# Last layer of a four-layer network: when the sums over the scan's states, and their additions into y, are due in the issue order

## The chip, the cores and the metric

The kernel runs on one core of a Trainium2 chip. The metric is the device time of one execution in microseconds (us); several executions are timed, and their median is given. The profile is of one more execution on the same kind of core. TensorE is called PE (its weight loads PEld), VectorE DVE, ScalarE ACT, GpSimd POOL, and SyncE, whose queue issues all DMAs here, SP.

## The reference, cut to what matters

Input and output are 4 images of 192 channels by 56 x 56 pixels in float32. Three layers (a windowed attention with dynamic kernels, a frequency-channel attention, an overlapping-window attention with a gated convolution) come first. The change lies in the fourth, a selective scan in four directions:

```python
xn = _ln_cf(x, ln_w, ln_b)
xz = jnp.einsum('dc,bchw->bdhw', in_proj_w, xn)
xc, z = jnp.split(xz, 2, axis=1)
...
xs = jnp.stack([x_hw, x_wh, x_hw[..., ::-1], x_wh[..., ::-1]], axis=1)
x_dbl = jnp.einsum('kcd,bkdl->bkcl', x_proj_w, xs)
dts, Bv, Cv = jnp.split(x_dbl, [R, R + N], axis=2)
dt = jax.nn.softplus(...)
# per direction, along l:
dA = jnp.exp(dt_t[..., None] * A)
h = dA * h + dt_t[..., None] * B_t[:, :, None, :] * u_t[..., None]
y = jnp.einsum('bkdn,bkn->bkd', h, C_t)
...
y = ...  # the four directions added, plus Ds * xs
out = jnp.einsum('cd,bdhw->bchw', out_proj_w, _ln_cf(y) * jax.nn.silu(z))
return x + out
```

Each of the 192 channels has 4 states (n). The sum over the states, `h * C` over n, and the adding of its result into y are what the change moves.

## The kernel before

Layer 3 (the last) works through 4 images, 4 directions and 7 chunks of 448 pixels: 112 steps t, in the order of the list `steps`, and each in two halves h of 96 channels, so 224 half-steps. 32 channels times 4 states fill the 128 partitions, so a half-step has three groups j. One half-step is, by line:

- `load` (L2289, L2295): SP loads the step's dt rows and, spread over the partitions, the B and C rows (`bc`, 8 buffers).
- `sizes` (L2310, L2322): PE projects dt, ACT takes the softplus. It is done for two steps at once.
- `decay` (L2348, L2356): SP spreads dt over the states into a `da` buffer (10 of them), three per half-step; ACT takes the exponential in place.
- `scan`: DVE multiplies dt by u to `du` (L2371 for rows, L2374 for columns, strided); PE replicates it over the states into three banks of PSUM (L2381); DVE multiplies each by B in place (L2387); DVE scans each (L2403), from `da`, the bank and the last value of the step before; POOL multiplies the states by C into `da` (L2410). Then PE sums over the states into one bank, three products with a matrix of zeros and ones (L2426), which frees the three `da` buffers; and DVE adds that bank into y (L2431 in the first direction, L2436 for rows, L2440 for columns).

Around it run `begin` (layer norm, projections and a 3 x 3 convolution of the next image: L2079 to L2224, with the convolution in L2167 and its silu in L2184), and `final` (layer norm of y, gate product on POOL L2245, output projection L2254, residual L2265, store L2268). The layer norm's lines L2079, L2081, L2089, L2094, L2097, L2098, L2100 serve both. Layer norm needs the exponential's table set on ACT, `begin` that of silu, `sizes` that of softplus; a switch is a table load (L357).

Nothing of the order is left to a scheduler after the build. Every one of these pieces is a Python generator, a thread of the class `Order`, and the program is written in the order in which `Order.run` picks their steps. A step announces, by `yield on_pe(...)`, `on_dve(...)` and so on, its engine, an estimated cost, the buffers that it takes, the table set that it needs and, with `ready`, a time at which its inputs are there. `Order.start` gives the earliest time at which a step could run by that model: the engine free, the buffers free, and `ready`, or where that isn't given the end of the thread's last step plus 0.25. `Order.run` issues the step with the least such time (plus 0.05 for each place behind in the plan), and sets the engine's, the thread's and the buffers' times by it. `order.end` is the modelled end of the step issued last. On the chip each engine then takes its own instructions strictly in that order, and semaphores hold an instruction until its inputs are there. So a due time decides only what stands in front of what in each engine's queue.

The steps of the change stand at the end of `scan`. `on_pe(600, "bank")` costs the three sums 1.14 and lets them be due 0.25 after the modelled end of POOL's last product; `on_dve(448)` lets the addition be due 0.25 after the sums. Modelled costs are in the model's microseconds, and enter the program as order alone. There are 8 banks of PSUM; `take` and `done` keep the model's account of them and of the buffers.

Of the kernel before, what the change touches and what calls it, by code (L numbers as in the profile page):

```python
# [42 lines left out]
NS, DTR, SCH = 4, 12, 448  # L43
# [222 lines left out]
def rows2(ap, w=W):  # L266
    return ap.rearrange("p (y x) -> p y x", x=w)


class Order:  # L270
# [29 lines left out]
    def take(self, kind="bank"):  # L300
        slot = min((s for s in self.kinds[kind] if s[0] is not None), key=lambda s: s[0])
        slot[0] = None
        return slot[1]

    def done(self, tile):

        (slot,) = (s for slots in self.kinds.values() for s in slots if s[1] is tile)
        slot[0] = self.end + self.LATENCY
# [57 lines left out]
def on_pe(n, *takes, ready=None):  # L366

    return "PE", 0.0019 * n, takes, None, ready


def on_pe_us(us, *takes, ready=None):
    return "PE", us, takes, None, ready


def on_dve(*n, takes=(), ready=None, each=0.00105):
    return "DVE", sum(0.08 + each * i for i in n), takes, None, ready


def on_scan(n, ready):
    return "DVE", 0.1 + 0.0023 * n, ("st",), None, ready  # L380
# [6 lines left out]
def on_pool(*n, each=0.0011, takes=()):  # L387
    return "POOL", sum(0.2 + each * i for i in n), takes, None, None
# [1601 lines left out]
def layer3(tc, order, pools, src, packs, aps, dst):  # L1990
# [80 lines left out]
    def gone(*what):  # L2071
        return what in passed
# [258 lines left out]
    def use(t, h):  # L2331

        users[t, h] = users.get((t, h), 0) + 1
        if users[t, h] == 2:
            done(sized[t][0][h])
# [23 lines left out]
    def scan(t, h):  # L2359

        b, o, s, c = steps[t]
        head = c == (NSC - 1 if s else 0)
        last = c == (0 if s else NSC - 1)
        px = slice(c * SCH, (c + 1) * SCH)
        yield lambda: t in sized and (2 * t + h == 0 or gone("multiplied", 2 * t + h - 1))
        dts, b_, c_ = sized[t]
        u = us[b % 2]
        yield on_dve(SCH, takes=("du",), each=0.0018 if o else 0.0015)
        du = take("du")
        if o == 0:  # L2370
            nc.vector.tensor_mul(du, dts[h], u[:HALF, h, px])  # L2371
        else:
            uv = u[:HALF, h].rearrange("p (y x) -> p x y", x=W)[:, 8 * c : 8 * c + 8]
            nc.vector.tensor_mul(rows2(du, H), rows2(dts[h], H), uv)  # L2374
        use(t, h)

        yield on_pe(500, *["bank"] * 3)
        tiles = [take() for _ in range(3)]
        for j in range(3):
            r = slice(32 * j, 32 * j + 32)  # L2380
            nc.tensor.matmul(tiles[j][:, :SCH], w["c96.rep"][r], du[r], start=True, stop=True)  # L2381
        done(du)
        passed.add(("multiplied", 2 * t + h))
        ends = []
        for j in range(3):
            yield on_dve(SCH, ready=order.end if j else None)
            nc.vector.tensor_mul(tiles[j][:, :SCH], tiles[j][:, :SCH], b_)  # L2387
            ends.append(order.end + order.LATENCY)
        if h == 1:
            done(b_)  # L2390
        das, sts = [], []
        for j in range(3):
            g = 3 * h + j
            yield lambda: (t, h, j) in decays and (head or (t - 1, g) in states)
            da, at = decays.pop((t, h, j))
            yield on_scan(SCH, ready=max(at, ends[j]))
            sts.append(take("st"))
            r = slice(None, None, -1 if s else 1)
            first = 0.0
            if not head:  # L2400
                before = states.pop((t - 1, g))
                first = before[:, 0:1] if s else before[:, SCH - 1 : SCH]
            nc.vector.tensor_tensor_scan(  # L2403
                sts[j][:, r], da[:, r], tiles[j][:, :SCH][:, r], first, ALU.mult, ALU.add
            )
            done(tiles[j])
            if not head:
                done(before)
            yield on_pool(SCH, each=0.0024)
            nc.gpsimd.tensor_mul(da, sts[j], c_)  # L2410
            das.append(da)
            if last:
                done(sts[j])
            else:
                states[t, g] = sts[j]
        if h == 1:
            done(c_)
            del sized[t]

        yield lambda: b == 0 or gone("read", b - 1, c if (o, s) == (0, 0) else 0)  # L2420
        yield lambda: (o, s) == (0, 0) or len(started) == 2 * NSC * (b + 1)
        yield lambda: s == 0 or o == 1 or added[b] >= 6 * NSC + 2 * (NSC - 1 - c) + h
        yield on_pe(600, "bank")
        py = take()
        for j in range(3):
            nc.tensor.matmul(py[32 * j : 32 * j + 32, :SCH], w["c128.sum"], das[j], start=True, stop=True)  # L2426
            done(das[j])
        yield on_dve(SCH)
        sums = py[:HALF, :SCH]
        if (o, s) == (0, 0):  # L2430
            nc.vector.scalar_tensor_tensor(  # L2431
                y[:HALF, h, px], u[:HALF, h, px], d_sum[:, h : h + 1], sums, ALU.mult, ALU.add
            )
            started.add((t, h))
        elif o == 0:
            nc.vector.tensor_add(y[:HALF, h, px], y[:HALF, h, px], sums)  # L2436
        else:

            yv = y[:HALF, h].rearrange("p (y x) -> p y x", x=W)[:, :, 8 * c : 8 * c + 8]
            nc.vector.tensor_add(yv, yv, sums.rearrange("p (x y) -> p y x", y=H))  # L2440
        done(py)
        added[b] += 1
        if o == 0 and s == 1 and h == 1:
            passed.add(("summed", b, c))
        if added[b] == 8 * NSC:
            passed.add(("scanned", b))
# [12 lines left out]
    for t in range(len(steps)):  # L2459
        add(2 * t - 5, load(t))  # L2460
        if t % 2 == 0:
            add(2 * t - 3, sizes((t, t + 1)))
        for h in range(2):
            add(2 * t + h - 1, decay(t, h))
            add(2 * t + h, scan(t, h))
# [59 lines left out]
```

## Time and profile before

| | |
|---|---|
| runs | 5719.17, 5724.87, 5725.76 us; median 5724.87 |
| profiled execution | 5731.28 us, of which 5729.5 us are the span from its first to its last instruction |
| mean granted PE clock | 0.929 |
| busy over the span | PE 85%, DVE 72%, ACT 46%, POOL 30% |
| layer 3's scans (L2403) | 672, of 1133 ns (1073 ns for the first of a row of chunks) |
| sums (L2426) | 1344 matmuls, two for each of the 672 products, from 4006.6 to 5705.7 us |
| additions (L2431, L2436, L2440) | 56 + 56 + 112, of 666, 607 and 607 ns |

The profile has, for each line of the program and each engine, the time that its instructions were busy and the time that the engine stood idle just before them, with what ended that wait. The waits by pair (who waited for whom) add up such idle times. A busy share is an average over the stretch it is given for; an engine that is full in a stretch sets the pace there, and idle time of another costs nothing by itself. In a row of the windows, the numbers after the instruction counts are PE's granted clock, the mean share of the DMA engines, and GB/s.

### The profile page before, as it was taken

To read this page: it belongs to the slowest core of one execution; us is meant where nothing else is said; L and a number is where in the kernel's file an instruction comes from. 1 tells how busy PE (TensorE), PEld (TensorE's weight loads), DVE (VectorE), ACT (ScalarE), POOL (GpSimd) and SP (SyncE) were. 2 spreads that over 40 slices of the span, in tenths; PEclk is the share of its full clock that TensorE was granted. 3 is DMA by queue.
4 is the path that set the end of the run, shared out by engine and by line. 5 is a ranking of instruction groups with operands and counts; after the bars stand their busy time and mean duration, and the time that the engine had idled before them with its cause. 6 is when DMAs were issued, how large, how long until landed. Compare 5 with 4: busy or idle time off the path is not lost. (4 is left out here: it accounts for less than half of the span.)

```text
span 5729.5 us, 137267 instructions
## 1 busy us (share of the span) xinstructions
PE 4866.4 (85%) x58114; PEld 2407.0 (42%) x58114; DVE 4140.6 (72%) x6600; ACT 2655.4 (46%) x4271; POOL 1699.9 (30%) x1688
## 2 busy tenths in 40 slices
PE   4988998998899687898898888868888888888777
PEld 2444554454454444555555555534332232222112
DVE  5788447544744026888988888883678999998997
ACT  0122323212232215555555555546776776676544
POOL 0000000000000013433333433321345555555564
PEclk9999998999999798999999999989998999999998
DMA  6132224333332521000000000002456656566654
GB/s 185 53 80 60 66 60 105 64 88 91 76 69 56 99 77 37 14 22 21 17 22 18 19 20 21 16 26 60 122 135 157 160 145 172 155 149 167 165 149 109
DMA packets 356373, 475.97 MB, mean 83 GB/s; under 512 B 43600, under 2 KB 354256, under 8 KB 355248
## 3 DMA queue, kind: packets, MB, share of 16 engines
q1 hardware_dynamic: 355760, 467.20, 32.9%
q8 instruction: 458, 7.50, 0.5%
q14 instruction: 155, 1.27, 0.1%
HBM read 249.73 MB, written 63.17 MB: 55 GB/s over the span
## 5 line engine op out<-in xcount | busy, mean ns | idle before, releaser
L2410 POOL TENSOR_TENSOR da<-st,bc 128x448 f32<-128x448 f32 x672 | 857.0, 1281 | 751.5 <-DVE st L2403 600.1
L731 PE MATMUL bank<-X,wu 64*49 64x392 f32 x6720 | 610.5, 509 | 89.2 <-DVE X L710 85.9
L2403 DVE TENSOR_TENSOR_SCAN st<-da,st,bank 128x448 f32<-128x448 f32 x576 | 646.3, 1133 | 4.3 <-POOL da L2410 1.8
L838 POOL TENSOR_TENSOR attn<-attn,rs 112x1568 f32<-112x1568 f32 (+1 forms) x24 | 67.1, 2795 | 1726.5 <-DVE rs L836 989.9
L2356 ACT ACTIVATE da<-da,a_neg 128x448 f32<-128x448 f32 x672 | 410.1, 659 | 161.9 <-DMA da<-dt 150.2
L357 ACT ACT_TABLE_LOAD x373 | 478.6, 1283 | 6.6
L2387 DVE TENSOR_TENSOR bank<-bank,bc 128x448 f32<-128x448 f32 x672 | 382.9, 618 | 83.4 <-PE bank L2381 78.2
L731 PEld LDWEIGHTS bank<-X,wu 64*49 64x49 f32 x6720 | 247.6, 123 | 416.1 <-issue 366.4
L2426 PE MATMUL bank<-da,w_c 128*32 128x448 f32 x1344 | 348.8, 575 | 85.3 <-POOL da L2410 66.3
L2381 PE MATMUL bank<-du,w_c 32*128 32x448 f32 x1344 | 291.1, 643 | 105.2 <-DVE du L2371 59.2
L1569 DVE SCALAR_TENSOR_TENSOR bxn<-bapad,w_b,bxn 96x448 f32<-96x448 f32 (+2 forms) x448 | 318.7, 756 | 0.0
L1026 ACT ACTIVATE hm<-bank,w_a 128x448 f32<-128x448 f32 x168 | 106.3, 633 | 435.6 <-PE bank L1017 428.2
L1032 PE MATMUL bank<-hm,w_a 128*96 128x448 f32 x672 | 285.1, 555 | 16.7 <-ACT hm L1026 16.6
L1017 PE MATMUL bank<-xc,w_a 128*128 128x448 f32 x672 | 283.4, 551 | 0.6 <-DVE xc L998 0.6
L1430 POOL TENSOR_TENSOR bsq<-bsq 128x448 f32<-128x448 f32 (+7 forms) x120 | 144.5, 1206 | 446.9 <-ACT bsq L1427 401.8
L678 ACT ACTIVATE q<-bank,qk_bias,qk_scale 128x280 f32<-128x280 f32 (+2 forms) x216 | 116.9, 544 | 294.4 <-PE bank L664 251.2
L2134 PE MATMUL bank<-row,w_c 128*96 128x448 f32 x448 | 206.5, 599 | 29.7 <-DVE row L2100 27.9
L1488 PE MATMUL bank<-bxn,w_b 128*96 128x336 f32 (+2 forms) x576 | 214.3, 498 | 19.0 <-DVE bxn L1440 16.7
L754 ACT COPY sm<-bank 128x392 f32<-128x392 f32 x96 | 43.0, 489 | 380.6 <-PE bank L731 368.2
L2381 PEld LDWEIGHTS bank<-du,w_c 32*128 32x128 f32 x1344 | 92.1, 199 | 299.7 <-DVE du L2371 76.0
L998 DVE SCALAR_TENSOR_TENSOR xc<-bank,w_a,xc 96x224 f32<-96x224 f32 x112 | 44.9, 441 | 226.3 <-PE bank L988 124.5
L1763 PE MATMUL bank<-bzpad,b_diag 32*32 32x224 f32 (+2 forms) x8064 | 182.7, 371 | 24.1 <-ACT bzpad L1735 12.7
(333 smaller groups left out, 10015.4 us busy)
## 6 DMA issues: line engine op xcount, KB each, us to landing
da<-dt SPq DMA_DIRECT2D x672, 224.0 KB
vb<-vmem SPq DMA_DIRECT2D x576, 98.0 KB
bc<-prod SPq DMA_DIRECT2D x224, 224.0 KB
xq<-x SPq DMA_DIRECT2D x132, 210.0 KB
xc<-x SPq DMA_DIRECT2D x56, 336.0 KB
row<-x SPq DMA_DIRECT2D x56, 336.0 KB
xs<-x SPq DMA_DIRECT2D x28, 336.0 KB
vmem<-vt SPq DMA_DIRECT2D x56, 168.0 KB
```

The source lines that it names most:

```text
L357: self.nc.scalar.preload_act_table_set(table)
L731: nc.tensor.matmul(pm[a][outs[i], : WIN * W].rearrange("p (y x) -> p y x", x=W), wu[halves[a], k, dx], xt[halves[a], :, i, dx : dx + W], s ...
L1017: nc.tensor.matmul(ph[:, :CH], w["a128.c1T"][:, k, 128 * m : 128 * m + 128], xt[:, k], start=(k == 0), stop=(k == 1),)
L1032: nc.tensor.matmul(acc[h][:HALF, :CH], w["a128.c2T"][:, m, HALF * h : HALF * h + HALF], hm, start=(m == 0), stop=(m == 5),)
L1488: nc.tensor.matmul(rows2(pq[:HALF, :m]), w["b128." + wn][:, k, HALF * h : HALF * h + HALF], out[:, k], start=(k == 0), stop=(k == 1),)
L1569: nc.vector.scalar_tensor_tensor(dst, x, wt[:, t : t + 1], dst, ALU.mult, ALU.add)
L2356: nc.scalar.activation(da, da, AF.Exp, scale=a_neg[:, k, g : g + 1])
L2381: nc.tensor.matmul(tiles[j][:, :SCH], w["c96.rep"][r], du[r], start=True, stop=True)
L2387: nc.vector.tensor_mul(tiles[j][:, :SCH], tiles[j][:, :SCH], b_)
L2403: nc.vector.tensor_tensor_scan(sts[j][:, r], da[:, r], tiles[j][:, :SCH][:, r], first, ALU.mult, ALU.add)
L2410: nc.gpsimd.tensor_mul(da, sts[j], c_)
L2426: nc.tensor.matmul(py[32 * j : 32 * j + 32, :SCH], w["c128.sum"], das[j], start=True, stop=True)
```

## The change

The sums' step gets a cost of 0.85 in place of 1.14, and is due 3.0 after the modelled end of the step issued when it is announced (as a rule POOL's last product) in place of 0.25. The addition is due 1.5 after the modelled end of the sums in place of 0.25. No instruction and no buffer is added. Since the model goes on from there, `da` buffers and banks are free later by its account, and everything behind is placed anew, on all five queues.

```diff
         yield lambda: s == 0 or o == 1 or added[b] >= 6 * NSC + 2 * (NSC - 1 - c) + h
-        yield on_pe(600, "bank")
+        yield on_pe_us(0.85, "bank", ready=order.end + 3.0)
         py = take()
         for j in range(3):
             nc.tensor.matmul(py[32 * j : 32 * j + 32, :SCH], w["c128.sum"], das[j], start=True, stop=True)
             done(das[j])
-        yield on_dve(SCH)
+        yield on_dve(SCH, ready=order.end + 1.5)
         sums = py[:HALF, :SCH]
```

Before, the waiting conditions ahead of the sums (three `yield lambda` lines) set the thread's time to the present one plus 0.25; a given `ready` takes the place of that as well.

## The prediction

> **What bounds the kernel now.** The edit touches layer 3 alone, so I first asked in which stretch of the span its lines run (the sums, L2426, start at 4006.6 us and end at 5705.7 us), and then which engine is full there. The table of windows, microseconds of the window and then busy time and instruction count of PE, PEld, DVE, ACT and POOL:
>
> ```profile
> 4000.00:4400.00 400.00, 345.83 (x2937) 120.40 (x2937) 303.43 (x389) 291.71 (x459) 181.28 (x156) 0.90 0.54 135
> 4400.00:5600.00 1200.00, 982.10 (x6102) 300.12 (x6101) 1102.60 (x1429) 769.99 (x1183) 678.60 (x545) 0.93 0.61 157
> 5600.00:5730.00 130.00, 91.39 (x266) 28.27 (x262) 93.95 (x119) 53.81 (x80) 57.18 (x43) 0.83 0.40 106
> ```
>
> Stretch A (4000 to 4400) is shared: PE is busy 86%, DVE 76%. In stretch B (4400 to 5600) DVE is busy 92% and everything else has room: DVE is the bound, and its 97 us of idle time are all that an order of issue can win there. Stretch C is the end. So the second view is what DVE waited for, 4000 us to the end (total us, times, longest):
>
> ```profile
> DVE bank L2387 <- PE bank L2381: 74.0, 73, 3.3
> DVE row L2081 <- PE bank L2079: 43.9, 27, 8.7
> DVE y L2440 <- PE bank L2426: 26.7, 19, 5.3
> DVE y L2431 <- PE bank L2426: 20.6, 7, 12.8
> DVE row L2265 <- PE bank L2254: 20.3, 13, 7.0
> DVE y L2436 <- PE bank L2426: 13.1, 9, 2.7
> ...
> DVE st L2403 <- ACT da L2356: 8.1, 6, 2.9
> ```
>
> The three additions into y wait 26.7 + 20.6 + 13.1 = 60.4 us for the sums. The same view for B alone has 9.7 + 2.5 + 9.9 = 22.1 us of this, and 47.0 us at L2387. The scans hardly wait for their decays (8.1 us).
>
> Third, PE's side. A group from the page, and how it looks in PE's timeline (start, duration, what, idle before it):
>
> ```profile
> L2426 PE MATMUL bank<-da,w_c 128*32 128x448 f32 x1344 | 348.8, 575 | 85.3 <-POOL da L2410 66.3
> ```
>
> ```profile
> 5644.63 0.91 PE L2426 MATMUL bank<-da,w_c 128*32 128x448 f32 x2
> 5645.75 0.94 PE L2426 MATMUL bank<-da,w_c 128*32 128x448 f32 x2 [0.21 <-POOL da L2410]
> 5647.85 0.94 PE L2426 MATMUL bank<-da,w_c 128*32 128x448 f32 x2 [1.16 <-POOL da L2410]
> ```
>
> PE has reached the three sums too early and stands between them until GpSimd has done its next product; whatever is behind them in PE's queue stands too. PE loses 66.3 us so (58.1 in B, by its waits there).
>
> Last, the loop that the edit lengthens. A `da` buffer is free once its sum has run; then SP reloads it, ACT takes the exponential, DVE scans. The waits of SP's queue and of ACT, from 4000 us on:
>
> ```profile
> SPq L2348 <- PE bank L2426: 157.6, 135, 4.8
> ```
>
> ```profile
> ACT da L2356 <- DMA da<-dt: 150.2, 81, 5.7
> ```
>
> SP's reloads hang on the sums 135 times: later sums mean later decays.
>
> **The change part by part.** No instruction's work is changed: both programs have 29528 PE, 6602 DVE, 1693 POOL and 2622 SP instructions (as the program lists them). ACT has 4299 instead of 4266: 33 more table loads, 24 of them in the last quarter of the exponentials, where softplus and exponential now alternate by one chunk instead of two. The rest is order, and it changes a lot after the first scans. I counted, in DVE's issue order, the work standing between a producer and its consumer, each instruction at its mean from the page and the group view (scan 1.13 us, L2387 0.617, L2374 0.971, L2371 0.852, additions 0.61 to 0.67, L2081 1.08, L2100 1.06, L2265 0.60).
>
> (1) Third scan to its addition: 3.77 us of work between on average before, 7.00 after. The shortest real distance in the trace's B is 2.24 us (product, sums, addition). Below it are 28 of 224 additions before, lacking 29.8 us in sum; after, 8, lacking 6.0: 80% goes. In B the wait is 22.1 us, so 17.7 go. The other 38.3 us are in A and C, mostly A, where PE is the fuller engine and the 12.8 us wait ended after 28 matmuls of the column projections (L2218, 10.65 us in the chain of waits) had kept PE, not after a product of GpSimd; I take one third, 12.8 us (bounds 0 and 38).
>
> (2) du to the first L2387. The lack at 1.1 us (shortest distance in B: 1.11) grows from 14.2 to 22.3 us, as du is no longer so often followed by an addition. But PE now issues the next replication (L2381) ahead of more sums: two replications of later half-steps stand before a sum 99 times of 224, against 2 times before. Counting also the sums that stand just ahead of a replication, the lack goes from 28.7 to 26.4 us, by 8%. Of the 74.0 us that is 6 us of gain. Bounds: a loss of 19 (at 1.5 us the plain count goes from 27.3 to 45.9) and a gain of 37 (the B waits without the 10.5 us where PE began at once after du).
>
> (3) The other waits of DVE for PE (L2081, L2265, L2100: 15 us in B, some 23 in C) sit behind the same PE queue, freed of up to 58 us of standing. I take 5 us, bounds 0 and 25.
>
> (4) The `da` loop. From an addition to the next scan that uses one of its buffers there are 17.8 us of DVE work before (least 10.5), 14.3 after (least 6.4); since the addition also stands about 1.25 us further behind its sums, the loop loses 2 to 3.5 us. In B the exponential ends 7 to 8 us before its scan starts (mean; a tenth of the third scans have under 2.1 us). Which of these are bound by the buffer? Those whose ACTIVATE waited for the DMA: 87 exponentials, with 9.95 us to spare in the mean, and only 3 of them under 2.25 us, lacking 2 us together. If only those move, the price is 2 us; if every exponential moves by 2.25 us, the largest lack of each half-step adds up to 47 us, at 3.5 us to 113. I take 8, near the low end, because the low slack of the others comes from ACT's own order, which is built anew.
>
> (5) Table loads: 33 x 1.283 us = 42.3 us on ACT, which is busy 770 of 1200 us in B. Work hides it: exponentials are early by the 7 us above. Uncovered, it would cost up to 42 us.
> The row: before the 193 loads from 4000 us on ACT idled 3.5 us in all, and the exponential follows at once. The Trainium skill (ScalarE: Activation LUTs, What ACT_TABLE_LOAD costs) speaks against this edit more strongly: 1283 ns and a drain of some 1380 ns, 2.66 us for each switch. By it ACT would pay 88 us and not 42, an estimate from that page; this trace shows the load but no such idle time around it, so the sum goes by 42, hidden.
>
> (6) Collisions of DVE and GpSimd. The contiguous du product takes 0.59 us or up to 2.59:
>
> ```profile
> L2371 DVE TENSOR_TENSOR du<-dt,u x112: 590/596/2593, 3980.6 to 5685.8; 96x448 f32<-96x448 f32 x112
> ```
>
> In the timeline 17 of the 26 long ones start while GpSimd runs the 2.1 us gate product of `final` (L2245, 28 in all) and make 25 of the 28 us lost; the others start under an L2410. After the edit a du that follows a scan and one other instruction, where L2410 still runs, is found 16 times, before 6; the three of them in the trace that met no other product lost 0.5 us in the mean, so 5 us more. Whether L2245 meets du more or less often, an order of issue doesn't tell: 28 x 1.5 us is the most it could cost, 25 us the most it could give back. I take 0 for both together (bounds 25 gained, 42 lost).
>
> SP's queue is rearranged too (bc, dr and row loads move among the `da` reloads); the bc loads wait for GpSimd and L2387 as before, and I take nothing for it. A bank is held some 1 to 2 us longer per half-step; PE waits on DVE for banks little (L2426 <- L2403, 10.8 us in B). POOL keeps the same products.
>
> Sum: -17.7 - 12.8 - 6 - 5 + 8 = -33.5 us. The profiled execution took 5731.3 us (span 5729.5 and 1.8 around it), so 5697.8; it is 6.4 above the median of the runs, 5724.9, and on the median's scale the forecast is **5691 us**.
>
> **The rivals.** *The decays come late* (slower). Mechanism: the sums free `da` later, SP reloads later, ACT waits and, being in order, holds up softplus and layer norm as well, so all exponentials move, not just the 87. It decides once that shift passes some 2.1 us, where the lack (37 us at 2.0, 47 at 2.25) equals the 41.5 us gained. At 3.0 us it costs 84: 5725 - 41.5 + 84 = 5767. For it: least loop distance 10.5 to 6.4, all ten buffers in turn; against it: 9.95 us to spare where the DMA was the last to come. 20%.
> *The wait only changes its name* (no difference): additions stop waiting, but L2387 waits 18.6 us more by the 1.5 us count, A gives nothing: -17.7 + 18.6 - 5 + 8 = +4, or -9 with A's third: about 5722. For it: du and L2387 stand closer. 18%.
> *PE's standing was behind everything* (much faster): all 60 us of additions, 37 us of L2387 and some 15 of the others go, 8 lost: about -104, half of it likely: 5621 to 5672. Against it: no L2387 wait of B falls directly after a stand of PE at GpSimd. 12%.
> That the edit does nothing is excluded by the order.
>
> **How the numbers follow.** Forecast 50%, its own range 5672 to 5712 by the bounds of (1) to (4). The range 5650 to 5760 takes in the third rival's near half, the second, and most of the first. About 0.2% (11 us) is what a measurement can tell from no change. Faster by more: 50 + 12 less a little = 60%. Within: 18%. Slower: 22%.
>
> **What would show it.** Right: the additions' waits for L2426 fall from 60 to under 30 us; L2426's wait for L2410 falls well below 66; DVE busy share in B above 93%; L2403 waits for L2356 under 20 us. Wrong: L2403 <- L2356 at 40 us or more with ACT <- DMA da grown (first rival); L2387 <- L2381 at 90 or more (second). ACT loads 33 tables more in any case. The forecast is also wrong if L2371's busy time itself moves by over 10 us through (6).

## The result, and the profile after

The change makes the kernel slower: 5792.52 us, the median of 4 runs (5784.43 to 5796.60), against 5724.06 (5719.17 to 5725.76): ratio 1.0121, interval 1.0106 to 1.0136. The forecast of 5691 had the wrong sign, and the time lies above the range's end of 5760. The profiled execution took 5795.22 us (span 5793.4), 63.9 more than that of before; the parts below are counted in these two.

The table of windows of the changed kernel, the same first two windows as before, the third up to its later end (columns: window, length, busy time and count of PE, PEld, DVE, ACT, POOL, then granted clock, DMA share, GB/s):

```profile
4000.00:4400.00 400.00, 344.08 (x2979) 119.82 (x2978) 319.36 (x409) 288.64 (x461) 186.35 (x164) 0.91 0.55 140
4400.00:5600.00 1200.00, 930.95 (x5946) 295.04 (x5943) 1053.01 (x1345) 783.67 (x1172) 620.69 (x514) 0.82 0.59 149
5600.00:5795.00 195.00, 126.63 (x380) 37.98 (x380) 145.98 (x185) 86.10 (x123) 86.13 (x67) 0.76 0.45 112
```

In the first window DVE does 16 us more than before. In the second, where DVE is the bound, it falls from 92% busy to 88%, with fewer instructions done. PE didn't become full there either. Its clock fell from 0.93 to 0.82.

What DVE waited for, from 4000 us to the end (total us, times, longest):

```profile
DVE bank L2387 <- PE bank L2381: 145.4, 116, 4.9
DVE row L2081 <- PE bank L2079: 44.3, 33, 4.7
DVE row L2265 <- PE bank L2254: 28.6, 18, 7.0
DVE row L2100 <- ACT bank L2098: 15.5, 12, 4.0
DVE y L2431 <- PE bank L2426: 14.5, 6, 11.4
DVE y L2440 <- PE bank L2426: 8.0, 9, 2.1
DVE st L2403 <- issue: 6.6, 9, 1.4
DVE y L2436 <- PE bank L2426: 2.8, 4, 1.8
DVE st L2403 <- ACT da L2356: 2.2, 3, 1.2
```

The three additions wait 25.3 us in place of 60.4, and the scans 2.2 for their decays in place of 8.1. One row takes back more than all of this: the product behind the replication, L2387, waits 145.4 us in place of 74.0.

Two PE groups of the page (busy, mean ns; idle before, and the releaser that ended most of it):

```profile
L2381 PE MATMUL bank<-du,w_c 32*128 32x448 f32 x1344 | 325.1, 726 | 285.3 <-DVE du L2371 154.0
...
L2426 PE MATMUL bank<-da,w_c 128*32 128x448 f32 x1344 | 273.2, 655 | 18.6 <-DVE st L2403 11.6
```

The standing at the sums is gone, as intended: before, 85.3 us with 66.3 at POOL's product. But the replication, whose idle time was 105.2 us before (its row then: 291.1 busy, mean 643), now has 285.3 in front of it. The waits of PE between 4400 and 5600 us name the releasers, first before the change, then after:

```profile
PE bank L2426 <- POOL da L2410: 58.1, 82, 3.0
PE bank L2381 <- DVE du L2371: 42.6, 27, 3.8
PE bank L2381 <- DVE du L2374: 34.2, 33, 2.9
```

```profile
PE bank L2381 <- DVE du L2371: 116.8, 41, 5.8
PE bank L2381 <- DVE du L2374: 83.6, 34, 5.4
```

Once past the sums, PE arrives at the next replication and stands there for du: 200.4 us in place of 76.8. I read some 58 of these 124 us as the old standing under a new name: totals can't be matched piece by piece, but PE would have had to wait for DVE, the bound, in any case. PE's timeline in the last image shows it (start, duration, what, idle before it), before and after; before, PE waits for du (0.41 us at 5462.42) even behind the last of the sums:

```profile
5455.55 1.03 PE L2381 MATMUL bank<-du,w_c 32*128 32x448 f32 x6 [0.93 <-DVE du L2374]
5456.50 0.94 PE L2426 MATMUL bank<-da,w_c 128*32 128x448 f32 x2
5459.51 0.94 PE L2426 MATMUL bank<-da,w_c 128*32 128x448 f32 x2 [2.07 <-POOL da L2410]
5461.08 0.94 PE L2426 MATMUL bank<-da,w_c 128*32 128x448 f32 x2 [0.63 <-POOL da L2410]
5462.42 1.03 PE L2381 MATMUL bank<-du,w_c 32*128 32x448 f32 x6 [0.41 <-DVE du L2374]
```

```profile
5456.51 1.87 PE L2381 MATMUL bank<-du,w_c 32*128 32x448 f32 x6 [5.24 <-DVE du L2374]
5458.31 1.71 PE L2426 MATMUL bank<-da,w_c 128*32 128x448 f32 x6
5459.96 1.22 PE L2310 MATMUL bank<-dr,w_c 64*96 64x448 f32 x4
5464.28 1.87 PE L2381 MATMUL bank<-du,w_c 32*128 32x448 f32 x6 [3.11 <-DVE du L2374]
```

Before, a half-step's sums came one by one between two replications, and PE's idle time was cut into pieces of 0.4 to 2.1 us. After, the three sums are done in one go behind the replication, and the idle time is one piece of 3 to 5 us; and the replication takes 1.87 us in place of 1.03. The granted clock goes with the longer matmuls: by its record it was half at 5456.5 and at 5464.3 us after, and full at both replications before. This is the page's row of the granted clock in 40 slices, before and after:

```profile
PEclk9999998999999798999999999989998999999998
```

```profile
PEclk9999999999998889999999999889988988998658
```

The three slices before the last read 8, 6 and 5 in place of 9, 9 and 9.

Where the 63.9 us arise, by images of 168 scans each (length in us / granted clock):

| | image 0 | 1 | 2 | 3 (last) | behind it |
|---|---|---|---|---|---|
| before | 491 / .89 | 419 / .94 | 420 / .94 | 382 / .91 | 28.0 |
| after | 470 / .90 | 443 / .87 | 444 / .89 | 411 / .66 | 33.8 |

Image 0, where PE is the fuller engine, gains 21 us; each later image loses 24 to 29, and the end 6.

### The profile page after: what moved, and what is told of

The parts are those of the page before. It is cut to its first block, busy times and chain, and to the rows that moved or that the text cites. A ratio compares the mean times of both kernels' runs of the same rounds, so it can differ in the third digit from the quotient of the medians.

```text
span 5793.4 us, 137143 instructions
## 1 busy us (share of the span) xinstructions
PE 4849.1 (84%) x58114; PEld 2407.3 (42%) x58114; DVE 4158.3 (72%) x6600; ACT 2698.3 (47%) x4304; POOL 1674.3 (29%) x1688
## 5 line engine op out<-in xcount | busy, mean ns | idle before, releaser
L2410 POOL TENSOR_TENSOR da<-st,bc 128x448 f32<-128x448 f32 x672 | 829.4, 1243 | 812.1 <-DVE st L2403 657.6
L2381 PE MATMUL bank<-du,w_c 32*128 32x448 f32 x1344 | 325.1, 726 | 285.3 <-DVE du L2371 154.0
L2387 DVE TENSOR_TENSOR bank<-bank,bc 128x448 f32<-128x448 f32 x672 | 387.5, 620 | 150.2 <-PE bank L2381 149.7
L2356 ACT ACTIVATE da<-da,a_neg 128x448 f32<-128x448 f32 x672 | 408.0, 658 | 139.6 <-DMA da<-dt 138.1
L2381 PEld LDWEIGHTS bank<-du,w_c 32*128 32x128 f32 x1344 | 98.2, 219 | 495.1 <-DVE du L2371 160.5
L2426 PE MATMUL bank<-da,w_c 128*32 128x448 f32 x1344 | 273.2, 655 | 18.6 <-DVE st L2403 11.6
L2134 PE MATMUL bank<-row,w_c 128*96 128x448 f32 x448 | 205.5, 599 | 19.3 <-DVE row L2100 17.9
```

Source lines behind the costliest of these rows:

```text
L2356: nc.scalar.activation(da, da, AF.Exp, scale=a_neg[:, k, g : g + 1])
```

## The experiments

Ratios are to the kernel before, run again beside each group (its medians were 5718.0 to 5720.4), with their intervals. Three theories stood at the start. *The model's account* (theory A): with later sums the model believes the `da` buffers and banks to be free later, and so places all else worse. *The clock* (B): the fused idle time of PE lowers its clock, and slower replications make DVE wait. *The sums' own place* (C): they now stand in front of later replications in PE's queue. Every kernel that changes a number of the model or of the buffers gets a whole new order.

**Two more `da` buffers, after (e1) and before (e2).** In each: `keep_late("da", [SCH], 10)` becomes

```diff
-        da=keep_late("da", [SCH], 10),
+        da=keep_late("da", [SCH], 12),
```

> The change, with 12 da buffers in place of 10. Theory A (the later due sums keep the 10 da buffers taken in the model's account; the decays and scans are placed later, less DVE work is left between du and the first multiply by B, and ACT switches tables more often): with 12 buffers the model is not short of them, the work between du and L2387 lacks 47 us at 2.0 us (80 after, 52 before), loads fall from 407 to 383, so L2387 <- L2381 falls from 145 to under 80 us and the time to 5680 to 5705, faster than before. Theory B (PE's clock: with its stands at the sums gone PE waits for du in one longer piece, the granted clock falls, and the way from du over the replication to the multiply gets longer): clock after 4400 us stays under 0.85, time 5765 to 5795. Theory C (the sums' own place in front of later replications): L2387 waits stay above 120 us, time 5760 to 5795.

Measured: 5758.11 us, 1.0065 (1.0045 to 1.0084). Last image 392 us at clock 0.70; L2387 waits 119.7 us.

> The kernel before, with 12 da buffers: the control of the run with 12 buffers and the change. If two more buffers are worth time by themselves: 5690 to 5715. By theory A they are not, as the scans wait for decays only 8 us; the order that the model makes of them even has more lack between du and L2387 (93 us at 2.0 us in place of 52): 5725 to 5765. Theories B and C say nothing of it; the clock in the last image should stay about 0.9.

Measured: 5778.92 us, 1.0104 (1.0079 to 1.0128): 60 us slower than before, though the sums are due at once. Its last image took 418 us at clock 0.72, where about 0.9 was expected. More buffers are not better by themselves, so the 34 us of e1 can't be put down to them.

**The model's account alone (e3).** The sums stay late, but the model is told that the `da` buffers are free as early as with prompt sums:

```diff
             done(das[j])
+            order.free(das[j], order.end - 2.2)
```

`free` is a new method that only sets the slot's time. It enters the model alone; semaphores guard the buffer as before.

> The change with 10 buffers, but the model is told that the da buffers are free when they were in the kernel before (2.2 earlier than the end of the sums); the chip's own waits are untouched. Theory A: the order is like that with 12 buffers (lack 47 us at 2.0, 373 loads, third scan to addition 7.35 us), so 5690 to 5720, with up to 20 us of waits of L2403 for decays that are late in fact. Theory B: clock low, 5765 to 5795. Theory C: 5760 to 5795. If what costs the time is that the real buffers come late: L2403 <- L2356 over 40 us and the time above 5780.

Measured: 5758.90 us, 1.0068 (1.0051 to 1.0085). L2387 waits 106.9 us, last image 391 us at 0.72. It gives back nearly half of the loss, like e1; whether by its mechanism or as another throw of the order was then open (see the scatter below).

**Idle products for the clock, three places (e4; e5, e6; e9 to e11).** Products whose results nobody uses keep PE active in the last image; no step of the computation is left out, and the model isn't told, so the order of all else stays. First, four ahead of the sums:

```diff
         py = take()
+        for _ in range(4 if b == B - 1 else 0):
+            nc.tensor.matmul(py[:HALF, :384], ones, inT[:, 0], start=True, stop=True)
```

> The change, with four idle products of PE (constant operands, written into the sums' bank before the sums) ahead of the sums of the last image alone, which keep PE busy. The order is otherwise the same. Theory B: the clock of the last image rises from 0.52 to above 0.8, L2381 -> L2387 waits in it fall, and most of the 28 us lost there come back: 5760 to 5775. Theories A and C: the clock may rise, but the waits hang on the order: 5785 to 5800.

Measured: 5826.92 us, 1.0186 (1.0171 to 1.0201). The clock of the last image rose to 0.90, but the image took 453 us: the sums now came behind the idle products, and the additions waited 54 us.

Then five behind the sums, into unused rows of the bank, in the changed kernel and in the one before:

```diff
+        for _ in range(5 if b == B - 1 else 0):
+            nc.tensor.matmul(py[HALF:, :384], w["c128.sum"], inT[:, 0], start=True, stop=True)
         yield on_dve(SCH, ready=order.end + 1.5)
```

> The change, with five idle products of PE (constant operands, into partitions of the sums' bank that nobody reads) behind the sums of the last image's half-steps, where PE next waits for du; the order of all else is untouched. If the low clock (0.66 in the last image, 0.91 before) is what costs the last image its 29 us: the clock there rises above 0.85, the replication takes 1.2 to 1.4 us in place of 1.78, the L2387 waits of the image that start with PE ready fall from 22 to about 8 us, and the image takes 390 to 398 us in place of 411; in all 5773 to 5781. If the order alone does it: image 408 to 418 us and 5788 to 5800 in all.

Measured: 5816.93 us, 1.0164 (1.0149 to 1.0180); image 443 us at 0.90.

> The same five idle products in the kernel before, whose last image already has a clock of 0.91: a control of what they cost where the clock has little to gain. 0 to 10 us more than before, 5718 to 5728; if it is 20 us or more, the idle products are themselves in the way and the run with the change and these is read against that.

Measured: 5823.16 us, 1.0174 (1.0159 to 1.0190); image 482 us. In e5 the clock rose, in e6 it had little to gain, and both images grew longer. The additions' waits of e5 and of e6 show one reason (L2429 is the idle product):

```profile
DVE y L2442 <- PE bank L2429: 23.1, 14, 3.0
```

```profile
DVE y L2442 <- PE bank L2429: 58.5, 28, 3.5
```

The additions waited for the idle products themselves, which write other rows of the same bank. So these three runs measure their own waits too.

Last, three ahead of the replication, into the bank that it then overwrites, so that nothing but PE itself waits for them:

```diff
+        for _ in range(3 if b == B - 1 else 0):
+            nc.tensor.matmul(tiles[0][:32, :384], w["c128.sum"], inT[:, 0], start=True, stop=True)
```

> The change, with three idle products of PE ahead of each replication of the last image, written into the bank that the replication then overwrites: they run while PE waits for du, and no addition waits for them (in the runs before it did). If PE's long idle pieces and the half clock behind them cost the last image time: its clock rises from 0.66 above 0.85, the replication falls from 1.78 to about 1.3 us, its L2387 waits from 30 to 12 to 18 us, and the image from 411 to 390 to 400 us; in all 5772 to 5782. If the low clock is only a sign of a slow order: clock up, image still 408 us or more, 5788 or more.

> The same three idle products in the kernel before, the control: its clock in the last image is 0.91, so little is to be won, and PE's idle pieces are short, so they can delay the replication. 5720 to 5745, the last image 382 to 402 us.

> The change, with three idle products ahead of each replication of the last image and two ahead of those of the other images. If the lost clock (0.87 to 0.89 in images 1 and 2, 0.94 before) makes their 24 us each: clock 0.93, images 1 and 2 at 430 us or less, 5745 to 5770 in all. If it is the sums that stand in front of the replication when du is done: the idle products add 0.6 us to a PE that is already late 20 to 30 times of 56, images 1 and 2 at 443 us or more, no gain on the run with the last image alone.

Measured: 5787.29 us, 1.0120 (1.0103 to 1.0137), for the changed kernel; 5749.35, 1.0055 (1.0035 to 1.0075), for the one before; and 5872.23, 1.0263 (1.0244 to 1.0282), for the changed one with three in the last image and two in each of the others. The windows of the last image, before the change, after it, and e9:

```profile
5319.00:5701.00 382.00, 279.33 (x871) 67.20 (x870) 362.20 (x472) 189.72 (x280) 228.77 (x174) 0.91 0.58 150
```

```profile
5349.00:5759.00 410.00, 276.05 (x869) 72.47 (x870) 369.69 (x470) 216.88 (x300) 211.59 (x174) 0.66 0.56 137
```

```profile
5342.00:5751.00 409.00, 321.27 (x1199) 92.57 (x1198) 369.84 (x471) 219.73 (x302) 212.20 (x174) 0.90 0.56 137
```

The clock is back (0.66 to 0.90), the three replicated banks take 1.25 us again in place of 1.78 (1.16 before the change), and the image takes as long as ever. Inside it the L2387 waits with PE ready at once fell from 22 to 11 us, and those with PE late (it began the replication after du was ready) rose from 7 to 22: an idle product in front of a replication delays it where du is already there. In the kernel before, where the clock had little to gain (0.91 to 0.95), the same products cost 30 us of the image. So a high clock alone doesn't bring the time back. How much the low one cost, this can't say: if it did cost time, the remedy cost about as much. The control e10 was itself 10 us longer in the last image than expected (412 against at most 402), and in e11 images 1 and 2 have a clock of 0.93 and 0.95 and still take 471 and 468 us.

**Each half of the change alone (e7, e8, e12).** The sums late and the addition as before:

```diff
-        yield on_dve(SCH, ready=order.end + 1.5)
+        yield on_dve(SCH)
```

> Half of the change: the sums due later (cost 0.85 and 3.0), the addition due as before. If the loss comes from the sums' place in PE's queue (ahead of later replications, held da buffers, PE idle in longer pieces): nearly all of it is here, 5770 to 5800, L2387 waits above 120 us, clock of the last image under 0.75, 416 table loads. If it comes from the addition's place on DVE: 5710 to 5735.

Measured: 5839.08 us, 1.0202 (1.0176 to 1.0229). The addition 1.5 later, the sums as before:

```diff
-        yield on_dve(SCH)
+        yield on_dve(SCH, ready=order.end + 1.5)
```

> The other half: the addition due 1.5 after the sums, the sums due as before. DVE work from the third scan to the addition is 4.75 us (3.77 before, 7.00 after), the lack between du and L2387 at 2.0 us is 66 (52 before, 80 after). If the sums' place carries the loss: 5700 to 5730, additions wait 35 to 50 us in place of 60, the clock as before. If the addition's place carries it: 5760 or more.

Measured: 5709.53 us, 0.9986 (0.9976 to 0.9996). DVE's waits from 4000 us on, the sums alone and then the addition alone:

```profile
DVE bank L2387 <- PE bank L2381: 117.2, 109, 3.5
DVE y L2440 <- PE bank L2426: 38.6, 37, 2.8
...
DVE y L2431 <- PE bank L2426: 30.6, 15, 12.4
```

```profile
DVE bank L2387 <- PE bank L2381: 85.7, 75, 3.0
...
DVE row L2265 <- PE bank L2254: 31.4, 15, 7.0
DVE row L2100 <- ACT bank L2098: 22.9, 16, 2.2
DVE y L2431 <- PE bank L2426: 10.5, 11, 3.2
DVE du L2371 <- ACT dt L2322: 10.0, 1, 10.0
DVE y L2440 <- PE bank L2426: 9.8, 7, 2.1
...
DVE y L2436 <- PE bank L2426: 1.5, 2, 1.3
```

This is the separation. The later addition alone takes the additions' waits from 60.4 to 21.8 us, as much as the whole change does, and raises L2387 little (85.7; 74.0 before). The later sums alone make L2387 wait 117 us and don't help the additions (80.7 us). So what the change wins at the additions comes from its second line, and the loss from its first. By images it is the same: e8 alone shortens image 0 (461 us; 491 before), and e7 alone makes images 1 to 3 longer by 33 to 39 us. Two limits: the halves don't add up (+119 and -11 us, together +68), and e8's gain in time is small, because most of the 38.6 us come back in other rows: L2265 waits 31.4 us in place of 20.3, L2100 22.9 in place of 6.3, one du 10.0, and L2387 11.7 more. With the addition due 3.0 later:

> The kernel before, with the addition alone due 3.0 after the sums (the sums due as before). Third scan to addition 6.55 us of DVE work, as in the change, lack between du and L2387 at 2.0 us 28 (52 before, 66 with 1.5), 373 table loads. If the additions' place is harmless and the sums' place alone does the harm: additions wait under 20 us, L2387 under 75, clock as before, 5670 to 5700. If an addition that stands late blocks banks or the scans: 5715 or more.

Measured: 5714.93 us, 0.9991 (0.9982 to 1.0000). No more to gain there; 5670 to 5700 was expected if the additions' place were worth its waits.

**The scatter of the order (f1 to f4).** Since every new number makes a new order, I changed one that says nothing: the due time by 0.1 to 0.2, the modelled cost of prompt sums by 5%.

```diff
-        yield on_pe_us(0.85, "bank", ready=order.end + 3.0)
+        yield on_pe_us(0.85, "bank", ready=order.end + 2.9)
```

> The change with 2.9 in place of 3.0 in the sums' due time: a step in the model far smaller than any latency on the chip, but the issue order comes out anew (lack between du and L2387 at 2.0 us 71 in place of 80, 409 table loads). If the loss belongs to sums that are due late: 5775 to 5810. If much of it is the luck of one order: it moves by 25 us or more, out of that range.

> The same with 3.2 (lack 68, in the last image 12 in place of 27, 409 loads). If the loss belongs to sums that are due late: 5765 to 5805, the last image nearer 392 than 411 us as its lack is smaller. If much is the luck of one order: outside.

Measured: 5753.21 us, 1.0060 (1.0042 to 1.0077), for 2.9 and 5767.66, 1.0088 (1.0073 to 1.0103), for 3.2.

```diff
-        yield on_pe(600, "bank")
+        yield on_pe(570, "bank")
```

> The kernel before with the sums' modelled cost 570 in place of 600 (1.08 in place of 1.14), due as before: the order comes out anew (lack 62 in place of 52, 366 loads). If the loss of the change belongs to the late due time, this stays near before: 5710 to 5735. If one order's luck is worth tens of us: 5745 or more, or 5695 or less.

> The kernel before with the sums' modelled cost 640 (1.22), due as before (lack 68, 378 loads). As the run with 570: 5710 to 5740 if the late due time makes the loss, further off if one order's luck does.

Measured: 5700.65 us, 0.9968 (0.9958 to 0.9979), for 570 and 5723.01, 1.0009 (1.0000 to 1.0018), for 640. So three orders with prompt sums lie from 5701 to 5723, three with sums due about 3.0 later from 5753 to 5793. The groups don't overlap (30 us between their nearest), but inside each the order alone moves 22 to 40 us. The other runs fit: with prompt sums e8, e12 and f6 (below) took 5694 to 5715 us, with late ones e1, e3 and e7 5758 to 5839. One doesn't: e2, prompt with two more buffers, took 5779, so an order can be as slow without late sums. The change's own 68 us are the far end of these three; its typical price is some 50 (medians 5768 and 5718). And the 34 us that e1 and e3 gave back lie within this scatter: they show nothing of the model's account.

**Half the delay (f5), and the better half with another cost (f6).**

```diff
-        yield on_pe_us(0.85, "bank", ready=order.end + 3.0)
+        yield on_pe_us(0.85, "bank", ready=order.end + 1.5)
```

> The change with the sums due 1.5 after POOL's product in place of 3.0; cost 0.85 and the addition's 1.5 as in the change. The orders with the sums due at once took 5701 to 5723 us, those with 2.9 to 3.2 took 5753 to 5793. If the loss grows with the due time: between them, 5725 to 5760, PE's idle pieces of 2 us and more in the last image between 15 and 30, its clock between 0.7 and 0.9. If a small delay is harmless and only one that comes up to the next replication hurts: 5700 to 5725.

Measured: 5741.39 us, 1.0036 (1.0022 to 1.0049), between the groups; last image 392 us at 0.77. Last, the kernel before with cost 570 for the sums and the addition due 1.5 later:

> The fastest order so far (the kernel before with the sums' cost 570) with the addition alone due 1.5 later. If the additions' place gains by itself (60 us of waits gone to some 20): 5680 to 5698. If the gain of 18 us with 570 was the luck of one order: it is lost in a new order, 5700 to 5725.

Measured: 5694.46 us, 0.9952 (0.9939 to 0.9965), which beats both kernels. Its waits of DVE and the window of its last image:

```profile
DVE bank L2387 <- PE bank L2381: 98.0, 83, 3.0
...
DVE y L2431 <- PE bank L2426: 4.6, 2, 3.2
...
DVE y L2440 <- PE bank L2426: 1.2, 1, 1.2
...
DVE y L2436 <- PE bank L2426: 0.3, 1, 0.3
```

```profile
5286.00:5673.00 387.00, 279.14 (x882) 67.87 (x881) 360.47 (x473) 192.59 (x284) 227.70 (x175) 0.90 0.59 147
```

The additions wait 6.1 us, and the clock stays at 0.90: the additions' waits can be removed without late sums. Of its 25 us, 18 are what f3 has by the cost alone, a throw of the order; the other 7 are less than the scatter. Nor does the total at L2387 rank the kernels by itself: it is 98.0 us here, in the fastest, and 91.7 in e2.

**PE's idle pieces and its clock, over all runs.** Counted from the traces in the last image, PE with its weight loads:

| sums due | kernels | idle pieces of 2 us and more | us at half clock |
|---|---|---|---|
| at once | before, e8, e12, f3, f4, f6 | 7 to 14 | 61 to 82 |
| 1.5 later | f5 | 25 | 177 |
| about 3.0 later | after, e1, e3, e7, f1, f2 | 24 to 39 | 218 to 276 |
| at once, 12 `da` buffers | e2 | 40 | 236 |

Few long pieces go with a high clock and many with a low one, in each kernel without idle products; e2, slow with prompt sums, is in the pattern of the late ones. But the total idle time separates these groups as well (96 to 106 us at once, 116 to 156 about 3.0 later), and f5 and the change, with 130 us idle and 25 and 24 such pieces each, have 177 and 276 us at half clock. So the pieces alone don't set it.

The traces' clock records show more. The clock isn't halved more often: 16 times in the last image before the change, 15 times after. What differs is how long the half clock lasts. With the sums due at once its longest stretch there is 7 to 10 us, with f5 20, with the late sums 24 to 171, with e2 48; after the change it is one of 170.7 us, from 5463.9 us on. Its reason, as far as the records tell it, is in the last section.

## Why the prediction was wrong

Times of the whole stretch from 4000 us on, of the two profiled executions:

| step | foretold | measured |
|---|---|---|
| (1) additions wait for the sums | -30.5 | -35.1 (60.4 to 25.3) |
| (2) L2387 waits for the replication | -6, bounds -37 and +19 | **+71.4** (74.0 to 145.4) |
| (3) L2081, L2265, L2100 | -5 | +17.9 (43.9 to 44.3; 20.3 to 28.6; 6.3 to 15.5) |
| (4) decays | +8 | -5.9 (8.1 to 2.2) |
| (5) table loads | 0, hidden | no wait found that needs them (see below) |
| (6) du beside POOL | 0 | +12.8 (L2371 +4.8, L2374 +8.0) |

Together +61 of the 63.9 us.

**The step that failed is (2)**: "the lack goes from 28.7 to 26.4 us, by 8%. Of the 74.0 us that is 6 us of gain." In its place +71.4 us were measured. That the late sums make this wait is shown by e7 (117 us) against e8 (86); how, the traces tell in part.

- It took PE's standing at the sums as harm to what is behind them. What was behind was mostly a replication that had to wait for du. PE's waits for du in front of L2381 grew by 124 us as the 58 us of standing went, and L2387 waits more, not less.
- It took the chain from du to the first replicated bank as fixed at 1.1 us, the shortest distance of the old trace. That is still the shortest after, but in the last image the chain is mostly longer: the first bank takes 0.98 us in place of 0.71 and all three 1.78 in place of 1.16. A distance measured at one clock was used for an order that has another.
- Its bound of +19 came from trying 1.5 us for the chain. A sharper doubt was at hand: by the same count at 2.0 us, the lack goes from 52 to 80. Even those 28 us are less than half of the 71. Nor does its own range, 5672 to 5712, follow "by the bounds of (1) to (4)": at their bad ends (-17.7, 0, +19, 0, and 47 for the decays) they add up to 5773.

How much of the 71 us the clock carries isn't settled. In the last image (29 us longer) some 30 half-steps stall at L2387; at 0.27 to 0.62 us more for each replication that is 8 to 19 us, by direct count. In images 1 and 2 (24 us longer each) the clock fell less, to 0.87 and 0.89, and the waits there with PE late rose from 18 to 30 and 32 us: other PE work stood in front of the replication. In image 0 they rose as much, from 23 to 39 us, with the clock unchanged (0.89 and 0.90), so there the order does it without the clock. How the rise of images 1 and 2 divides stays open; e11, meant to tell, added its own work to the queue.

The other steps. **(1)** was right, in size and in place: from 4400 to 5600 us the additions' waits fell from 22.1 to 6.3 us (17.7 foretold to go), elsewhere from 38.3 to 19.0 (12.8). By e8 it is the work of the second line alone. **(3)** assumed PE to be freed, which it was not; 9 of its 18 us are L2100 behind ACT, on which the 33 more table loads of **(5)** (373 to 406, as foretold) lie. But they aren't needed for it: e8, e12 and f6 have 194, 193 and 184 loads from 4000 us on (193 before), and L2100 waits 22.9, 16.9 and 21.7 us there. So nothing here speaks against hidden loads. **(4)** was wrong in sign but small. In **(6)** the contiguous du moved 4.8 us, within the bound; the strided one, which it had not looked at, moved 8.0 us. Its group (shortest, median and longest in ns, then when), before and after:

```profile
L2374 DVE TENSOR_TENSOR du<-dt,u x112: 946/970/1012, 4134.5 to 5574.9; 96x448 f32<-96x448 f32 x112
```

```profile
L2374 DVE TENSOR_TENSOR du<-dt,u x112: 948/974/1671, 4127.4 to 5627.5; 96x448 f32<-96x448 f32 x112
```

The shortest and the median hardly change, the longest goes from 1012 to 1671 ns: a few of them, counted in the last section, are held up for long.

The rivals. *The decays come late*: refuted. SP waits longer for the sums (157.6 to 215.0 us), but ACT waits less for its reloads (150.2 to 138.1) and the scans less for ACT. *The wait only changes its name*: this was the right place, and its mark of 90 us at L2387 was passed with 145.4. Its price, 18.6 us, was a quarter of the true one, so that it ended at no difference. *PE's standing was behind everything*: refuted, and with it the belief that the forecast shared in part. Of the marks, the additions (25 us), the sums' wait for POOL and the decays came out as foretold; DVE's share above 93% did not (88%), and that was the one that stood for the time.

## What to carry to other kernels

An engine that stands in its queue for a result loses nothing by it if what comes next would have waited too: before moving the standing instruction back, look up what the instruction behind it waits for. If only the consumer was too early (the additions on the bound engine), move the consumer and leave the producer; here the addition alone got all that the change won at the additions. That is still no gain in time by itself: where the bound engine meets other waits soon after, most of it comes back there. And where an issue order is made by a model, change a number that says nothing first: the scatter of the order, 22 to 40 us here, is the least that a difference must exceed before one order against another shows a cause.

## What the runs showed of the hardware

- The granted clock follows how busy PE was in the 3.4 us before. In the clock records of these traces it is 1 or 0.5, in pieces that are whole multiples of 3.41 us. I counted such windows in all 20 profiled runs, from 4000 us to the last scan, with the busy time of PE's matmuls. After a window at full clock with PE busy for less than 40%, the next was at half clock in all 747 cases; at 60% or more, in 137 of 6449. After a window at half clock with PE busy for less than 80%, the clock never came back (652 cases); at 97% or more it did in 1035 of 1119. So idle pieces of about 2 us can be enough to halve the clock, and it takes a much fuller window to get it back: in the last image 35 of 81 windows at half clock were under 80% after the change, 1 of 20 before. In images 1 and 2, pieces of 1.5 us and more go from 9 in each to 20 and 23, PE's idle time from 60 us to 76 and 85, and the clock from 0.94 to 0.87 and 0.89. The Trainium skill (TensorE: Matmul & The Clock Gate, The HAM clock gate) says that the clock is halved after an idle window of about 3.4 us. The window's length agrees; but of the 1188 halvings counted only 195 came after an idle stretch of that length, so here a window need not be idle, only less than about half full.
- Where a strided du product on DVE and a product by C on POOL (L2410) meet, the one that starts first keeps its pace. Before, all 112 strided du products (L2374) ran before a POOL instruction that started beside them: they took 0.97 us, and POOL's product 1.80, where one that met none of them takes 1.13. After, 20 of them started under a running POOL instruction and took 1.36 us in the mean and 1.67 at most; the other 92 still took 0.97. Each of the 20 ended 0.84 to 0.87 us after POOL's instruction did, so it hardly advanced beside it.
